# ScalarE's order inside a graph-attention step: the scalings of one chunk ahead of the exponentials of the next, and outputs one slot later

## The chip, the core and the metric

The kernel runs on one NeuronCore of one Trainium2 chip. The metric is the time on the device of one execution, in microseconds (us). A NeuronCore has five engines, each with its own queue that it works through in order: TensorE (PE: matrix products; PEld is the loading of its stationary operand), VectorE (DVE), ScalarE (ACT), GpSimd (POOL) and SyncE (SP). They meet only at semaphores. An engine whose next instruction waits holds up everything behind it in its own queue, and nothing else directly.

## The reference, cut to what matters

The input is `x`, 8 graphs of 2048 nodes with 128 features each, and one adjacency matrix of 2048 x 2048 with about 16 neighbours in a row. Four layers follow each other. Layers 0 and 1 are transformer layers whose attention is masked by the adjacency. Layers 2 and 3 are graph-attention (GAT) layers, and the change is in these:

```python
h = x @ W
s_i = h @ a_src
s_j = h @ a_dst
e = s_i[:, :, None] + s_j[:, None, :]
e = jnp.where(e >= 0, e, NEG_SLOPE * e)
e = jnp.where(adj[None, :, :] == 0, -jnp.inf, e)
att = jax.nn.softmax(e, axis=-1)
out = jnp.einsum('bij,bjd->bid', att, h)
y = out + x
mu = jnp.mean(y, axis=-1, keepdims=True)
var = jnp.mean((y - mu) ** 2, axis=-1, keepdims=True)
return ln_gamma * (y - mu) * jax.lax.rsqrt(var + LN_EPS) + ln_beta
```

For each node: a leaky-ReLU score for every neighbour, a softmax over the neighbours, the weighted sum of their rows `h`, the residual, and a layer norm.

## The kernel before, in words

**Lists and tables.** The adjacency is turned once into lists of neighbours. Nodes are sorted by their number of neighbours and cut into 16 tiles of 128 nodes (one a partition); tile t has `CAPS[t]` places for neighbours, from 30 down to 11, 277 in all. Each layer has a table in DRAM with one row a node: for a GAT layer the 8 graphs' `h` (8 x 128 values) and 8 scores `s_j`, 4128 bytes. One gather (line 296, an indirect DMA that POOL issues) brings one neighbour of each of 128 nodes into a buffer, so a GAT layer makes 277 gathers.

**Chunks.** A tile's neighbours are cut into chunks of 3 or 4 (`ns`; one chunk has 2), 75 chunks a GAT layer. A chunk's gathers fill one of `KVB = 6` buffers and are issued `AHEAD = 3` chunks early. The generator `gat_chunk` works off one chunk in five stages, divided by `yield`:

1. PE makes the scores `e` in one of three banks of PSUM (tag `m`): lines 654, 658, 662, the last of which reads the gathered `s_j` and so waits for the chunk's DMAs. ACT then makes two small exponentials of them, `wa` (line 667) and `wb` (line 668).
2. DVE takes the larger of the two as the weights, twice: line 670 into PSUM (`pair`) for itself and line 675 into SBUF (`ws`) for ACT.
3. The rows are scaled by their weights: DVE does 6 of the 8 graphs in one instruction (line 681), ACT the other two (`SCALED = 2`), in 2 x ns small instructions (line 686).
4. DVE folds the chunk's neighbours in half by one addition (line 690).
5. PE adds what is left into the tile's sums `acc`, with matmuls against the identity (line 696, four of 512 columns).

**Tails.** When a tile's last chunk is added, `sums` makes the softmax denominators, and `tail` starts a generator that passes some slots, divides on DVE (`outputs`, line 565, which reads `acc` and writes `o`), and starts two `gat_tail`s, one for each half of the graphs, the second three slots after the first. A `gat_tail` advances one `yield` a slot: PE makes the residual sum `y` (lines 706, 710, 714); `normed` takes ACT squares (line 404), a power on POOL (line 409, the reciprocal root), and, two slots after the squares, four ACT products (line 413). In layer 2 four PE transposes follow (line 305), one slot later an ACT copy (line 723), and one slot later `project`: PE makes the rows of the next table from the copy (lines 444, 450, 454, 459), and one slot later ACT copies them out (lines 464 to 466); when both halves are done, POOL scatters the rows into layer 3's table (`put_rows`, line 417). In layer 3 DVE applies the last gain and offset instead (lines 731, 732), and POOL scatters the result to the output (line 734).

**The order.** No scheduler moves anything: the kernel is recorded under a manual schedule, so each engine's queue holds its instructions in the order in which this Python code makes them. The loop in `layer` runs one iteration a chunk, i. For a GAT layer an iteration fetches chunk i+3, runs stage 1 of chunk i+1, stage 3 of chunk i-1, a slot, stage 2 of chunk i, a slot, stages 4 and 5 of chunk i-2, and a slot. `slot()` advances every tail by one step. So the order of an engine's queue in one iteration is: on PE, scores (i+1), tail steps of two slots, sums (i-2), tail steps of the third slot; on ACT, exponentials (i+1), scalings (i-1), tail steps of all three slots; on DVE, line 681 (i-1), lines 670 and 675 (i), line 690 (i-2), with `outputs` after that in the third slot; on POOL, the gathers (i+3), then the powers and scatters of the tails.

Of the kernel before, what the change touches and what calls it, by code (L numbers as in the profile page):

```python
# [51 lines left out]
def pieces(t, n):  # L52

    res, k = [], 0
    for m in split(CAPS[t] if t > 0 else BASE, n):
        res.append((k, m, False))
        k += m
    if t == 0:
        res.insert(1, (BASE, FOLD, True))
    return res  # L60
# [3 lines left out]
def sparse_path(ctx: ExitStack, tc: tile.TileContext, ins: dict, out: bass.AP, flag: bass.AP):  # L64
# [19 lines left out]
    def misc():  # L84
        return pm.tile([P, 512], F32, tag="m", name="m")
# [289 lines left out]
    def folded_sums(w, box):  # L375

        columns = w.shape[-1]
        ps = misc()[:, :columns]
        for i in range(FOLD):
            nc.tensor.matmul(ps, merge, w[:, i, :], start=i == 0, stop=i == FOLD - 1)  # L380
        box["folded"] = small.tile([P, columns], F32, tag="folded", name="folded", bufs=1)
        nc.scalar.copy(box["folded"], ps)
# [261 lines left out]
    def gat_chunk(l, c):  # L644
        box, t, k, ns = c["box"], c["t"], c["k"], c["ns"]
        if k == 0:
            box["acc"] = pacc.tile([P, NB // 4, 512], F32, tag="acc", name="acc")
            at, n = (0 if t % 2 == 0 else 512 - NB * CAPS[t]), CAPS[t]
            box["w"] = pair[:, at : at + NB * n].rearrange("p (s b) -> p s b", b=NB)
        acc, w = box["acc"], box["w"]  # L650
        hs = c["buf"]
        e = misc()[:, : ns * NB].rearrange("p (s b) -> p s b", b=NB)
        at = first[t] + k
        nc.tensor.matmul(
            e, ident_bf, lmask_bf[:, at : at + ns, None].to_broadcast([P, ns, NB]),
            start=True, stop=False,
        )
        nc.tensor.matmul(
            e, spread if c["folded"] else ident, s_own[:, t, None, :].to_broadcast([P, ns, NB]),
            start=False, stop=False,  # L660
        )
        nc.tensor.matmul(e, ident, hs[:, :, NB * D :], start=False, stop=True)  # L662

        wc = w[:, k : k + ns, :]
        wa = small.tile([P, 4, NB], F32, tag="wa", name="wa", bufs=3)
        wb = small.tile([P, 4, NB], F32, tag="wb", name="wb", bufs=3)
        nc.scalar.activation(wa[:, :ns, :], e, AF.Exp)  # L667
        nc.scalar.activation(wb[:, :ns, :], e, AF.Exp, scale=SLOPE)  # L668
        yield
        nc.vector.tensor_max(wc, wa[:, :ns, :], wb[:, :ns, :])  # L670
        if c["folded"]:
            box["wf"] = small.tile([P, FOLD, NB], F32, tag="wf", name="wf", bufs=1)
            nc.vector.tensor_max(box["wf"], wa[:, :ns, :], wb[:, :ns, :])
        ws = small.tile([P, 4, SCALED], F32, tag="ws", name="ws", bufs=3)
        nc.vector.tensor_max(
            ws[:, :ns, :], wa[:, :ns, NB - SCALED :], wb[:, :ns, NB - SCALED :]
        )
        yield
        hv = hs[:, :, : NB * D].rearrange("p s (b c) -> p s b c", b=NB)
        nv = NB - SCALED  # L680
        nc.vector.tensor_mul(  # L681
            hv[:, :, :nv, :], hv[:, :, :nv, :], wc[:, :, :nv, None].to_broadcast([P, ns, nv, D])
        )
        for i in range(ns):
            for b in range(nv, NB):
                nc.scalar.mul(hv[:, i, b, :], hv[:, i, b, :], ws[:, i, b - nv : b - nv + 1])  # L686
        yield
        left = -(-ns // 2)
        if ns > 1:
            nc.vector.tensor_add(hv[:, : ns - left], hv[:, : ns - left], hv[:, left:ns])  # L690
        yield
        if c["folded"]:
            folded_sums(box["wf"], box)
        for i in range(left):
            for j in range(NB // 4):
                nc.tensor.matmul(  # L696
                    acc[:, j, :], merge if c["folded"] else ident, hv[:, i, 4 * j : 4 * j + 4, :],
                    start=k + i == 0, stop=c["last"] and i == left - 1,
                )
        yield  # L700
# [230 lines left out]
    def advance(group):  # L931
        for g in list(group):
            if next(g, 0) == 0:
                group.remove(g)

    def slot():
        advance(threads)
        advance(tails)
# [5 lines left out]

    def tail(l, t, box):
        def rest():
            for _ in range(2 if l < 2 else 3):
                yield
            outputs(l, t, box)
            part = attention_tail if l < 2 else gat_tail  # L950
            tails.append(part(l, t, box, 0))
            tails.append(later(3, lambda: part(l, t, box, 4)))
            yield

        tails.append(rest())

    def later(n, make):
        for _ in range(n):
            yield
        yield from make()  # L960

    def layer(l):
        boxes = [{} for _ in range(NT)]
        att = l < 2
        per = 2 if att else 4
        chunks = []
        for t in range(NT):
            for k, ns, folded in pieces(t, per):
                chunks.append(dict(t=t, k=k, ns=ns, folded=folded, box=boxes[t], last=False))
            chunks[-1]["last"] = True  # L970
        n = len(chunks)

        def fetch(c):
            if c >= n:
                return
            c = chunks[c]
            c["buf"] = buffer()[:, : c["ns"] * width(l)].rearrange("p (s c) -> p s c", s=c["ns"])
            for i in range(c["ns"]):
                gather(l, first[c["t"]] + c["k"] + i, c["buf"][:, i])

        def state(t):
            if t < NT:
                if l == 0:
                    threads.append(fetch_state(t, boxes[t]))
                else:
                    boxes[t].update(x=load_state(t), ready=True)

        for box in boxes:
            box["state"] = state

        def begin(t):
            if att:
                threads.append(attention_begin(l, t, boxes[t]))

        if l == 0:
            threads.append(find_lists(0))
            state(0)
            drain()
        for i in range(AHEAD):
            fetch(i)  # L1000
        if l > 0:
            state(0)
        drain()
        begin(0)
        drain()
        if l == 0:
            threads.append(find_lists(1))
        run = [(attention_chunk if att else gat_chunk)(l, c) for c in chunks]

        def go(i, times=1):  # L1010

            if 0 <= i < n:
                for _ in range(times):
                    next(run[i], None)

        def is_last(i):
            return 0 <= i < n and chunks[i]["last"]

        def end(i):
            t = chunks[i]["t"]  # L1020
            tail(l, t, chunks[i]["box"])

        if not att:
            go(0)
        for i in range(n + 2):
            fetch(i + AHEAD)
            if i < n and chunks[i]["k"] == 0:
                t = chunks[i]["t"]
                if l == 0 and t + 2 < NT:
                    threads.append(find_lists(t + 2))  # L1030
                if t == 0:
                    state(1)
                    threads.append(later(12, lambda: state(2) or iter(())))
                while att and "asked" not in chunks[i]["box"]:
                    advance(threads)
            if i + 2 < n and chunks[i + 2]["k"] == 0:
                begin(chunks[i + 2]["t"])
            if att:

                go(i - 2)  # L1040
                if is_last(i - 2):
                    end(i - 2)
                go(i)
                slot()
                go(i)
                slot()
                if is_last(i - 1):
                    sums(l, chunks[i - 1]["t"], chunks[i - 1]["box"])
                go(i - 1, 2)
                slot()  # L1050
            else:


                go(i + 1)
                if is_last(i - 1):
                    sums(l, chunks[i - 1]["t"], chunks[i - 1]["box"])
                go(i - 1)
                slot()
                go(i)
                slot()  # L1060
                go(i - 2, 2)
                if is_last(i - 2):
                    end(i - 2)
                slot()
        if l == 3:
            verdict()
        drain()
# [530 lines left out]
```

## Time and profile before

| what | us |
|---|---|
| four runs | 3474.96, 3484.71, 3486.73, 3487.9; median 3485.72 |
| the profiled execution, its own time | 3481.77 |
| its span on the core (first to last instruction) | 3480.0 |
| busy in the span: DVE / PE / POOL / ACT | 3032.7 / 2827.8 / 2113.1 / 1450.3 |
| layer 2, first line 670 to last line 690 | 2343.0 to 2869.9 |
| layer 3, the same | 2921.0 to 3443.0 |

The first row is what a change is measured against; the profile is of one further execution. Layers 0 and 1 take the time before 2340 us, and the change does not touch them. Between the two GAT layers and after the second lie some 50 and 37 us in which the last tails run out and the next table is written.

In the lists of waits, "A <- B: t, n, m" says that instructions of line A stood idle t us in all before they started, n times, m us at most, and that B was the last thing they waited for; "issue" is idle time that ended with no event the profile shows. A timeline row gives the start, the duration, engine, line, operation, tiles and shapes, a count if several are merged, and in brackets the idle time before it. The figures of windows are busy times of each engine in a stretch; PEclk is the share of full TensorE clock that was granted.

### The profile page before, as it was taken

What the parts mean: (1) busy time and instruction counts of PE and PEld (TensorE: products, weight loads), DVE (VectorE), ACT (ScalarE), POOL (GpSimd) and SP (SyncE); (2) the same over time, 40 slices, a digit from 0 to 9 for tenths busy, and PEclk for the clock granted to TensorE, in tenths of its full rate; (3) what the DMA queues carried; (4) which work ended last, traced back from release to release, by engine and by line L of the source; (5) the groups of instructions that cost most, each with busy time, mean ns of one, the idle gap of its engine ahead of it and who ended that gap; (6) DMA issues with size and microseconds to landing.
All of it is one profiled execution on the core that took longest, in us unless ns stands there. A gap on an engine that the chain in (4) does not pass through costs nothing. (4 is left out here: it accounts for less than half of the span.)

```text
span 3480.0 us, 36421 instructions
## 1 busy us (share of the span) xinstructions
PE 2827.8 (81%) x11364; PEld 1676.2 (48%) x11364; DVE 3032.7 (87%) x2545; ACT 1450.3 (42%) x5142; POOL 2113.1 (61%) x1441
## 2 busy tenths in 40 slices
PE   5657888889899966888888999967898896877786
PEld 4423454455555542445555555653555554444443
DVE  8789999999999929999999999928777773988886
ACT  5712333344444430223333434444555553444454
POOL 0054666666666433655677766528877755888874
PEclk9879999999999989989999999988999997889888
DMA  8486788888787557777887887728998865888883
GB/s 338 181 304 247 276 298 302 322 289 306 296 318 292 195 198 269 275 300 280 302 313 293 303 304 291 258 96 282 318 311 307 321 215 203 293 305 291 293 274 123
DMA packets 195892, 955.38 MB, mean 275 GB/s; under 512 B 33778, under 2 KB 35572, under 8 KB 124080
## 3 DMA queue, kind: packets, MB, share of 16 engines
q0 software_dynamic: 172352, 859.22, 68.6%
q1 hardware_dynamic: 18434, 75.51, 5.7%
q10 hardware_dynamic: 4904, 18.24, 1.4%
q8 instruction: 93, 1.52, 0.2%
q14 instruction: 109, 0.89, 0.1%
HBM read 934.86 MB, written 85.07 MB: 293 GB/s over the span
## 5 line engine op out<-in xcount | busy, mean ns | idle before, releaser
L296 POOL DMA_INDIRECT kv<-table,lists x1108 | 1612.9, 1456 | 549.0 <-issue 228.2
L546 PE MATMUL acc<-kv,ident 128*128 128x512 f32 x2200 | 1105.9, 633 | 260.7 <-DVE kv L536 260.2
L546 PEld LDWEIGHTS acc<-kv,ident 128*128 128x128 f32 x2200 | 411.9, 201 | 699.1 <-issue 365.8
L522 DVE TENSOR_TENSOR kv<-kv,q 128x2048 f32<-128x2048 f32 (+1 forms) x282 | 629.3, 2231 | 71.4 <-DMA kv<-table,lists 64.0
L525 DVE TENSOR_REDUCE sc<-kv 128x128 f32<-128x2048 f32 (+1 forms) x284 | 634.1, 2233 | 9.4
L409 POOL TENSOR_TENSOR rs<-ss,half 128x4 f32<-128x4 f32 x192 | 321.4, 1674 | 516.9 <-ACT n L404 510.4
L536 DVE TENSOR_TENSOR kv<-kv,w 128x2048 f32<-128x2048 f32 (+1 forms) x284 | 631.4, 2223 | 0.0
L696 PE MATMUL acc<-kv,ident 128*128 128x512 f32 x1184 | 601.9, 656 | 14.3 <-DVE kv L690 13.5
L404 ACT ACTIVATE n<-m,eps 128x128 f32<-128x128 f32 x768 | 271.5, 369 | 479.4 <-PE m L628 219.0
L681 DVE TENSOR_TENSOR kv<-kv,pair 128x3072 f32<-128x3072 f32 (+1 forms) x150 | 465.2, 3101 | 0.0
L531 ACT ACTIVATE w<-sc,lmask 128x64 f32<-128x64 f32 x554 | 164.4, 348 | 528.9 <-DVE sc L525 412.3
L690 DVE TENSOR_TENSOR kv<-kv 128x2048 f32<-128x2048 f32 (+1 forms) x150 | 296.6, 1978 | 84.0 <-ACT kv L686 62.9
L696 PEld LDWEIGHTS acc<-kv,ident 128*128 128x128 f32 x1184 | 238.9, 213 | 268.4 <-issue 227.3
L686 ACT ACTIVATE kv<-kv,ws 128x128 f32<-128x128 f32 x1108 | 339.0, 397 | 0.1
L413 ACT ACTIVATE n<-m,rs 128x128 f32<-128x128 f32 x768 | 218.3, 368 | 101.7 <-POOL rs L409 101.1
L667 ACT ACTIVATE wa<-m 128x32 f32<-128x32 f32 (+1 forms) x150 | 29.4, 196 | 485.0 <-PE m L662 424.9
L662 PE MATMUL m<-kv,ident 128*128 128x32 f32 (+1 forms) x300 | 62.2, 290 | 169.1 <-DMA kv<-table,lists 158.6
L404 ACT ACTIVATION_READ_ACCUMULATOR n<-m,eps 128x1 f32 x768 | 159.4, 208 | 0.0
L670 DVE TENSOR_TENSOR pair<-wa,wb 128x32 f32<-128x32 f32 (+1 forms) x150 | 29.8, 199 | 145.8 <-ACT wb L668 118.2
L628 PE MATMUL m<-w_L_w,hT 128*128 128x128 f32 x1024 | 156.3, 275 | 0.0
L417 POOL DMA_INDIRECT table<-rows,perm x48 | 78.0, 1625 | 111.6 <-ACT rows L441 51.1
L305 PE MATMUL m<-ident,n 128*128 128x128 f32 x640 | 108.7, 288 | 32.6 <-ACT n L413 30.2
(217 smaller groups left out, 3531.2 us busy)
## 6 DMA issues: line engine op xcount, KB each, us to landing
kept<-xT SPq DMA_DIRECT2D x48, 512.0 KB
xT<-kept SPq DMA_DIRECT2D x48, 512.0 KB
kv<-table,lists POOLq DMA_INDIRECT x1108
kv<-in_adj_dram SPq DMA_DIRECT2D x16, 1024.0 KB
table<-kv ACTq DMA_DIRECT2D x16, 1024.0 KB
kv<-in_x_nodes_dram SPq DMA_DIRECT2D x16, 512.0 KB
found<-cand POOLq DMA_DIRECT2D x16, 64.0 KB
table<-rows,perm POOLq DMA_INDIRECT x48
```

Source lines behind the costliest of these rows:

```text
L296: nc.gpsimd.indirect_dma_start(out=dst, out_offset=None, in_=tables[l][:, :], in_offset=bass.IndirectOffsetOnAxis(ap=lists[:, at : at + 1] ...
L404: nc.scalar.activation(dst[:, i, :], z[:, i, :], AF.Square, bias=eps, scale=D**-0.5, accum_out=ss[:, i : i + 1],)
L409: nc.gpsimd.tensor_tensor(rs, ss, half, op=ALU.pow)
L413: nc.scalar.mul(dst[:, i, :], z[:, i, :], rs[:, i : i + 1])
L522: nc.vector.tensor_mul(kk, kk, q[:, None].to_broadcast([P, ns, NB, D]))
L525: nc.vector.tensor_reduce(sc[:, :ns].rearrange("p s (b h) -> p (s b) h", h=NH), kk.rearrange("p s b (h j) -> p (s b) h j", h=NH), axis=AX. ...
L536: nc.vector.tensor_mul(vv, vv, w[:, k : k + ns, :].rearrange("p s (b h) -> p (s b) h", h=NH)[:, :, None, :] .to_broadcast([P, ns * NB, HD, ...
L546: nc.tensor.matmul(acc[:, j, :], merge if c["folded"] else ident, kv[:, i, 4 * j : 4 * j + 4, D:], start=k + i == 0, stop=c["last"] and i ...
L681: nc.vector.tensor_mul(hv[:, :, :nv, :], hv[:, :, :nv, :], wc[:, :, :nv, None].to_broadcast([P, ns, nv, D]))
L686: nc.scalar.mul(hv[:, i, b, :], hv[:, i, b, :], ws[:, i, b - nv : b - nv + 1])
L690: nc.vector.tensor_add(hv[:, : ns - left], hv[:, : ns - left], hv[:, left:ns])
L696: nc.tensor.matmul(acc[:, j, :], merge if c["folded"] else ident, hv[:, i, 4 * j : 4 * j + 4, :], start=k + i == 0, stop=c["last"] and i = ...
```

## The change

Two edits in what a GAT step does, and the calls that follow from them.

```diff
         nc.tensor.matmul(e, ident, hs[:, :, NB * D :], start=False, stop=True)
+        yield
 
         wc = w[:, k : k + ns, :]
...
-            for _ in range(2 if l < 2 else 3):
+            for _ in range(2 if l < 2 else 4):
                 yield
             outputs(l, t, box)
...
         if not att:
-            go(0)
+            go(0, 2)
...
                 go(i - 1)
+                go(i + 1)
                 slot()
                 go(i)
                 slot()
```

Stage 1 is cut in two: the scores on PE, and the exponentials on ACT. An iteration now runs the scores of chunk i+1, stage 3 of chunk i-1, the exponentials of chunk i+1, and then its slots. ACT's queue so has the scalings (line 686) ahead of the exponentials (lines 667, 668); PE's, DVE's and POOL's stages keep their places. And a GAT tile's `outputs` waits for four slots instead of three. It started in the third slot of an iteration; now it starts in the first slot of the next one. Every step of a GAT tail follows it by one slot. No instruction is added or removed, and no operand changes. Lines behind 663 get a number higher by one.

## The prediction

> **What bounds the kernel now.** The change touches only layers 2 and 3, so I read the profile by stage: first the windows of the two layers, then who waits for whom in each, then the timeline of one iteration. Windows (columns: busy us and count of PE, PEld, DVE, ACT, POOL; clock; DMA share; GB/s):
>
> ```profile
> 2343.00:2870.00 527.00, 455.27 (x1877) 268.46 (x1878) 420.41 (x381) 281.83 (x1150) 388.06 (x310) 0.93 0.84 293
> 2921.00:3443.00 522.00, 411.49 (x1277) 216.16 (x1277) 456.85 (x438) 253.40 (x1051) 413.49 (x325) 0.88 0.83 281
> ```
>
> No engine is full in either layer, so the waits decide. Waits of layer 2, first PE's, then DVE's, then ACT's longest (three lists of the same window):
>
> ```profile
> PE m L662 <- DMA kv<-table,lists: 34.7, 16, 6.7
> PE m L305 <- ACT n L413: 29.1, 23, 2.0
> ...
> PE m L305 <- ACT kv L686: 1.9, 3, 1.0
> ```
> ```profile
> DVE kv L690 <- ACT kv L686: 33.3, 19, 2.1
> DVE o L565 <- PE acc L696: 26.8, 12, 5.9
> DVE kv L690 <- issue: 9.8, 7, 2.1
> ```
> ```profile
> ACT wa L667 <- PE m L662: 196.4, 61, 7.7
> ```
>
> PE's busy 455 plus 35 for gathers plus 31 for ACT (29.1 + 1.9) is 521 of 527 us: **layer 2 is paced by PE**. 26 of the 35 us fall before 2430 us, while the first gathers fill up. DVE's idle 106 us are slack behind PE. In layer 3 it is POOL: busy 413, and its gathers have a further gap between them:
>
> ```profile
> POOL kv L296 <- issue: 57.3, 190, 1.7
> POOL rs L409 <- ACT n L404: 14.0, 6, 4.8
> ```
>
> The 57.3 us are 190 gaps of 0.3 us; the other gathers have the same gap under other names (some 30 us more). With the waits on ACT that is over 510 of 522 us. PE waits 91.3 us for gathers there: they come as fast as POOL issues them.
>
> One iteration of layer 2, from the timeline:
>
> ```profile
> 2617.60 0.18 PE L654 MATMUL m<-lmask_bf,ident_bf 128*128 128x32 bf16 x1
> ...
> 2618.28 0.20 ACT L667 ACTIVATE wa<-m 128x32 f32<-128x32 f32 x1 [2.46 <-PE m L662]
> 2618.29 1.05 PE L450 MATMUL m<-w_L_h,xT 128*128 128x128 f32 x8
> 2618.37 0.19 ACT L668 ACTIVATE wb<-m 128x32 f32<-128x32 f32 x1
> 2618.45 1.85 ACT L686 ACTIVATE kv<-kv,ws 128x128 f32<-128x128 f32 x6
> ...
> 2619.21 1.03 PE L459 MATMUL m<-w_L_h,xT 128*128 128x2 f32 x8
> ...
> 2620.20 1.12 ACT L413 ACTIVATE n<-m,rs 128x128 f32<-128x128 f32 x4
> ...
> 2621.38 1.11 PE L305 MATMUL m<-ident,n 128*128 128x128 f32 x4 [1.13 <-ACT n L413]
> ```
>
> Read it as a loop: PE makes scores; ACT, which had stood 2.46 us for them, runs its exponentials, then 1.85 us of scalings (2.44 for chunks of four), then the tail's products L413; PE waits for these with the transposes L305, and the sums L696 stand behind L305. The scalings were ready to run during the 2.46 us.
>
> **The change, part by part.** Sums are against the profiled execution's own 3481.8 us; the median of the runs shown is 3.9 us above.
>
> *1. L305's wait, layer 2: -31 us.* L413 loses 1.85 to 2.44 us of scalings ahead of it, and by the slot's shift L305 now stands behind L696 (eight passes, 3.44 us where the clock is full). Either alone covers a wait of 2.0 us at most. That the scalings fit in front: step by step in the trace, L667's idle time is longer than the block of L686 behind it in 62 of layer 2's 73 steps and in 47 of layer 3's; where it is not, the exponentials come up to 2.4 us later. Nobody is waiting for them there: L670 reads them an iteration later. The weights `ws` that L686 needs are always done, by 6.5 us at least before the present start of the exponentials.
>
> *2. A new wait, layer 2: +22 us.* The slot's shift also moves the copy L723 from the third slot (before the next scores) to the first (behind the next exponentials), and `project` reads that copy on PE right after the scores. From the rows: L654 starts at 0, exponentials at 0.68, ACT's next instruction at 0.85, the copy takes 0.60 and ends at 1.45; L450 starts 0.69 now and would start at about 1.5. That is 0.8 us for each of 28 halves in the window. Behind the waiting L450 stand L459, the sums L696 and the next scores; POOL's gathers wait for the buffers that L696 frees. Bounds: 0 if ACT runs far ahead, and 1.2 us a half (34 us) if `project`'s PSUM bank, which is that of the scores, holds back L444 too. I take 0.8, since each of its parts is a row.
>
> *3. DVE's waits: -3 us.* L690's waits (43 us) and L565's (27 us) go: L686 is done before the exponential that L670 waits for, and `outputs` stands 3.3 us (one L681) later. Both are hidden behind PE, whose L696 waits only 3.1 us for L690. What can come off is those 3 us; the bound is the 70 us in which DVE would be late if PE weren't.
>
> *4. TensorE's clock, layer 2: 0, between -10 and +10.* Three neighbouring windows round the L305 wait shown above:
>
> ```profile
> 2617.70:2621.10 3.40, 2.55 (x24) 2.42 (x22) 2.19 (x4) 2.82 (x12) 2.60 (x4) 1.00 0.91 317
> 2621.10:2624.50 3.40, 3.12 (x7) 1.92 (x8) 3.40 (x2) 1.41 (x5) 1.32 (x1) 0.51 0.96 342
> 2624.50:2627.90 3.40, 3.40 (x16) 1.88 (x15) 0.40 (x2) 0.38 (x3) 1.60 (x2) 0.99 0.84 284
> ```
>
> The clock halves for 3.4 us round a wait of 1.13 us, which costs up to 1.7 us. The old waits are longer (1.27 us each), the new ones more (28 for 23) and amid small matmuls; six windows either way are the 10 us. The Trainium skill (TensorE: Matmul & The Clock Gate, "What's actually happening") has the clock fall after an idle window of about 3.4 us; by it neither the old nor the new waits would touch the clock, and this term would be 0 without bounds. The row shows a halving with PE busy 2.55 of the 3.4 us before, so the bounds stay.
>
> *5. POOL and the buffers: -5 us.* In layer 2 POOL waits 23.4 us for L696 to free buffers; L696 comes ahead of L305 in two iterations a tile, but behind the new wait in two. The scatter L417 goes behind four gathers, and its wait of 7.4 us for ACT goes. Half of these 7.4 us, and 1 us of the rest: -5, between 0 and -15.
>
> *6. Layer 3: -4 us.* There is no L723 and no L305, so part 2 has no counterpart. POOL's gathers keep their number and length. What can go are its waits for ACT, 14.0 for L404 and 2.8 for L667: squares move a slot later but lose the scalings ahead of them. A quarter of 17; bounds -15, and +6 if the later slot makes the powers later. L731 and L732 move behind L681, 3.3 us later; their scatter L734 stands at least 5.0 us behind them in the layer now, so it is covered.
>
> *7. The ends: +1 us.* One slot more of the last tile but one runs after each loop. The `y` matmuls, one slot later, find `o` done: its new end is that of the present next L681, before or at their present start in every tile of layer 2's loop.
>
> Sum: -31 + 22 - 3 + 0 - 5 - 4 + 1 = -20. Parts 1 and 5 partly count the same time (a PE that is earlier frees buffers earlier anyway), so I take **-16**: 3466 on the profiled execution's terms, and 3468 against the runs, whose median is a little above it.
>
> **Rivals.**
>
> *A, larger gain:* DVE's and ACT's waits were what kept gathers late, so most of the 43 us of L690 goes too. For: the layer's DMA share is only 0.84. Against: L696 waits 3.1 us for L690. 3482 - 45 = 3437.
>
> *B, nothing:* L450's wait takes L305's place in full. This decides from 31 / 28 = 1.1 us a half, against my 0.8; with layer 3 at 0, 3482 to 3485. For it: the PSUM bank.
>
> *C, slower:* the copy comes later than I have it, because ACT is still in the scalings when the scores are done: those are now in front of the exponentials and the copy. If it costs 2 us a half, layer 2 gets 56 - 31 = 25 us longer, and with the clock's 10 some 35: 3517. It decides from 1.1 us a half too, and B ends where C begins. For: the full tail iterations, where ACT has squares and copies in the third slot. Against: 62 of 73 steps with room.
>
> *D, the change doesn't do what it says:* the built program's order shows L686 ahead of L667 and L305 behind L696, so I give it none.
>
> **How the numbers follow.** Forecast 0.48, A 0.13, B 0.25, C 0.14. The forecast's own spread is 3452 to 3478 by the bounds of parts 2, 4 and 5. About 0.3%, 10.5 us, is what a measurement of this kernel can tell from no change: faster is under 3475, slower over 3496. Faster: 0.40 of the forecast, A, and nothing else, 0.53. Same: the rest of the forecast, most of B, 0.31. Slower: C and 0.02 of B, 0.16. The range 3436 to 3496 takes in the forecast, A and B, and leaves C out.
>
> **What would show it.** L305's wait gone; L450 <- ACT L723 new, about 0.8 us x 28 in layer 2; L690 <- L686 and L565 <- L696 gone; L670 <- L668 not grown; layer 2 some 12 us shorter, layer 3 about the same. I am wrong if PE's waits in layer 2 sum to what they did, if the clock of layer 2 (0.93) moves by more than 0.02, or if layer 3 moves by more than 15 us.

## The result, and the profile after

The changed kernel takes 3487.82 us in the median (3479.45 to 3503.68, 41 runs), the kernel before 3485.52 (3472.18 to 3497.91, 67 runs): a ratio of 1.0008, 95% interval 1.0002 to 1.0014. The change moves nothing that matters. The profiled execution after took 3482.28 us, with a span of 3480.5.

Layer 2, from the first line 671 to the last line 691, went from 526.8 to 520.8 us; layer 3 from 522.0 to 522.5. Layer 2 began 4.3 us later though nothing ahead of it was changed (it began between 2340.0 and 2347.5 us in every kernel below but e20). With 1.4 us more between the two layers, this takes up the 6 us by which layer 2 is shorter. Each kernel has one profiled execution, and layer 3 took 522.5 to 533.7 us in four kernels whose layer 3 is the same (after, e21, e24 and e26). So single layers are read below to some 10 us, and kernels by their ratios. The windows of layers 2 and 3 after (columns as before):

```profile
2347.00:2868.00 521.00, 453.94 (x1857) 266.77 (x1856) 417.06 (x381) 287.48 (x1149) 397.35 (x311) 0.93 0.85 295
2921.00:3443.00 522.00, 403.14 (x1275) 214.47 (x1275) 450.23 (x435) 253.22 (x1047) 417.77 (x325) 0.89 0.83 281
```

PE is busy 454 us where it was busy 455, at the same clock of 0.93: nothing was won there. What PE waited for in layer 2:

```profile
PE m L662 <- DMA kv<-table,lists: 44.8, 26, 6.2
PE m L450 <- ACT xT L724: 6.1, 10, 0.6
PE m L444 <- ACT wb L669: 5.1, 9, 1.0
PE m L662 <- issue: 4.1, 3, 2.9
...
PE m L305 <- ACT n L413: 1.2, 1, 1.2
```

The wait of the transposes is gone, 31.0 to 1.2. In its place stand `project`'s waits, 15.6 us with the smallest rows (for the copy at L450; at L444 for a bank that the exponentials free, which are later now), and a longer wait for gathers, 48.9 us with the row marked "issue" where it was 36.4. Idle on PE in all: 71.7 before, 66.9 after. That is an exchange, not a gain.

The part of the gathers' wait in which the layer starts up is the same, 25.8 us before (up to 2430 us) and 25.5 after (up to 2434). The rest grew from 10.6 to 23.4. The same two rows behind the start-up, before and then after:

```profile
PE m L662 <- DMA kv<-table,lists: 8.9, 7, 2.0
PE m L662 <- issue: 1.7, 3, 1.2
```
```profile
PE m L662 <- DMA kv<-table,lists: 19.3, 17, 2.2
PE m L662 <- issue: 4.1, 3, 2.9
```

Issuing the gathers also kept GpSimd busy 19 us longer, for the same number of them (groups of layer 2, before and after; behind the count stand busy us and mean ns):

```profile
L296 POOL DMA_INDIRECT kv<-table,lists x269 | 329.5, 1225 | 105.3 <-issue 55.0 <-PE acc L696 23.4 <-PE m L658 9.1
L296 POOL DMA_INDIRECT kv<-table,lists x270 | 348.4, 1290 | 102.0 <-issue 60.2 <-PE acc L697 27.1 <-ACT wb L669 2.7
```

### The profile page after: what moved, and what is told of

The parts are those of the page before. It is cut to its first block, busy times and chain, and to the rows that moved or that the text cites. A ratio compares the mean times of both kernels' runs of the same rounds, so it can differ in the third digit from the quotient of the medians.

```text
span 3480.5 us, 36448 instructions
## 1 busy us (share of the span) xinstructions
PE 2817.8 (81%) x11364; PEld 1672.5 (48%) x11364; DVE 3023.9 (87%) x2545; ACT 1456.9 (42%) x5142; POOL 2134.5 (61%) x1441
## 5 line engine op out<-in xcount | busy, mean ns | idle before, releaser
L296 POOL DMA_INDIRECT kv<-table,lists x1108 | 1638.8, 1479 | 541.2 <-issue 237.9
L691 DVE TENSOR_TENSOR kv<-kv 128x2048 f32<-128x2048 f32 (+1 forms) x150 | 296.0, 1973 | 1.3 <-ACT kv L687 1.3
L671 DVE TENSOR_TENSOR pair<-wa,wb 128x32 f32<-128x32 f32 (+1 forms) x150 | 29.8, 199 | 249.9 <-ACT wb L669 155.6
L668 ACT ACTIVATE wa<-m 128x32 f32<-128x32 f32 (+1 forms) x150 | 29.4, 196 | 350.9 <-PE m L662 314.8
L662 PEld LDWEIGHTS m<-kv,ident 128*128 128x128 f32 x300 | 49.5, 208 | 204.1 <-issue 168.3
L628 PEld LDWEIGHTS m<-w_L_w,hT 128*128 128x128 f32 x1024 | 135.0, 192 | 0.0
```

The lines of the kernel that those rows point to most:

```text
L296: nc.gpsimd.indirect_dma_start(out=dst, out_offset=None, in_=tables[l][:, :], in_offset=bass.IndirectOffsetOnAxis(ap=lists[:, at : at + 1] ...
L628: nc.tensor.matmul(y[:, j, :], hT[:, f, j, :], wt["2"][:, f, :], start=False, stop=f == 1, skip_group_check=True,)
```

## The experiments

Three theories stood first. **T1**: GpSimd's queue of gathers paces both layers, so nothing on PE matters. **T2**: TensorE paces layer 2, and `project`'s new wait took the place of the transposes'. **T3**: the two edits cancel, and each alone does much. Later ones are **P** (the copy's wait is what the slot's shift costs) against **O** (the earlier half of the tail, outputs to powers, is), **G** (GpSimd's gathers hold the changed kernel back, in a second form because late sums reach their queue through the buffers), and **K** (the cost is TensorE's clock) against **W** (the waits themselves).

All runs in one table. Each ratio is to runs of the kernel before that were taken with it (medians 3483 to 3488), so rows are compared by their ratios; e4, e5 and e23 rest on two runs each. The last four columns are us of layer 2 in the profiled execution: its length, PE's busy and idle time, which add up to it, and the time at half clock in the stretches that begin in it. One more such stretch, begun before the layer, covers its first 15 to 19 us in each run, 35 in e3.

| kernel | us (median) | ratio to before, 95% | layer 2 | PE busy | idle | half |
|---|---|---|---|---|---|---|
| before | 3485.5 | 1 | 526.8 | 455.2 | 71.7 | 51 |
| after | 3487.8 | 1.0002 to 1.0014 | 520.8 | 453.9 | 66.9 | 55 |
| e1 order only | 3458.5 | 0.9896 to 0.9928 | 498.6 | 442.4 | 56.1 | 38 |
| e2 slot only | 3601.1 | 1.0304 to 1.0332 | 644.6 | 530.1 | 114.5 | 229 |
| e3 half the sums | 3449.3 | one run | 499.2 | 374.1 | 125.1 | 137 |
| e4 before, fewer gathers | 3409.1 | 0.9748 to 0.9794 | 504.3 | 447.9 | 56.4 | 38 |
| e5 after, fewer gathers | 3369.4 | 0.9662 to 0.9701 | 470.2 | 433.9 | 36.3 | 17 |
| e10 after, copy first | 3477.2 | 0.9975 to 0.9996 | 511.9 | 451.0 | 60.9 | 61 |
| e11 late half shifted | 3471.2 | 0.9954 to 0.9986 | 513.1 | 449.5 | 63.6 | 48 |
| e26 early half shifted | 3489.8 | 1.0003 to 1.0027 | 520.8 | 448.3 | 72.4 | 61 |
| e24 after, copy unread | 3474.4 | 0.9962 to 0.9986 | 510.3 | 444.7 | 65.6 | 51 |
| e28 slot only, copy unread | 3482.2 | 0.9979 to 1.0008 | 515.4 | 451.3 | 64.1 | 61 |
| e20 slot only, filled | 3560.4 | 1.0190 to 1.0229 | 561.3 | 504.0 | 57.3 | 31 |
| e23 slot only, half filled | 3557.4 | 1.0178 to 1.0230 | 584.4 | 506.0 | 78.4 | 106 |
| e21 after, filled | 3483.8 | 0.9979 to 0.9999 | 516.9 | 457.6 | 59.3 | 38 |
| e22 before, filled | 3493.4 | 1.0003 to 1.0026 | 530.1 | 473.6 | 56.5 | 34 |
| e16 after, rows reversed | 3482.2 | 0.9982 to 1.0018 | 515.4 | 452.5 | 62.9 | 55 |
| e17 order, rows reversed | 3459.5 | 0.9935 to 0.9972 | 500.5 | 439.2 | 61.3 | 31 |
| e18 before, rows reversed | 3483.6 | 0.9992 to 1.0018 | 527.5 | 457.7 | 69.8 | 58 |
| e19 e10, rows reversed | 3477.6 | 0.9973 to 1.0001 | 507.7 | 446.6 | 61.1 | 51 |

Layer 3 lay between 522 and 534 us in all of them but e4 and e5, with no order among the edits: the kernel before with only layer 2 edited (e22) had 529.

### One edit at a time, and each engine's load

e1 keeps the `yield` and the calls `go(0, 2)` and `go(i + 1)`, and undoes the slot; e2 is the reverse.

```diff
-            for _ in range(2 if l < 2 else 4):
+            for _ in range(2 if l < 2 else 3):
```

> The scalings go ahead of the exponentials, outputs stay in the third slot. Theory T1 (POOL's queue of gathers paces both GAT layers, so time saved on ScalarE and TensorE is slack): within 0.1% of before, layer 2 within 6 us of 527. Theory T2 (TensorE paces layer 2, and in the full change the wait of project for the copy took the place of the transposes' wait): here the copy stays in the third slot, so there is no such wait, the transposes' wait of 31 us shrinks to under 5, and the time falls by 15 to 30 us. Theory T3 (the two edits cancel): this one is faster by 10 us or more.

> Outputs one slot later, the order on ScalarE as before. The copy now stands behind the scalings: by the rows of before, project on TensorE waits 2.9 us a half, 81 us in layer 2. T1: some of that hides behind the gathers, layer 2 grows by 0 to 40 us. T2: layer 2 grows by 81 - 31 = 50 us. T3: the time grows by 10 us or more, as much as the order alone gains.

e3 and e4 lighten one engine of the kernel before:

```diff
-        for i in range(left):
+        for i in range(1):
...
-                    start=k + i == 0, stop=c["last"] and i == left - 1,
+                    start=k + i == 0, stop=c["last"],
```

> Before, with only the first of a chunk's two row sums added by TensorE (line 696), so half of its summing matmuls in the GAT layers is left out: TensorE loses 130 us in each of layers 2 and 3. T1: layer 2 loses under 25 us and layer 3 under 10, since the gathers go on as they were. T2: layer 2 loses 50 us or more.

```diff
-            for i in range(c["ns"]):
+            for i in range(c["ns"] - (l > 1 and c["ns"] == 4)):
```

> Before, with the fourth gather of each chunk of four left out in the GAT layers (53 of 277 a layer; the chunk is worked off with what lies in the buffer). T1: POOL loses 53 x 1.55 = 82 us a layer, and both layers get shorter by 40 us or more, until TensorE (486 us with its waits in layer 2) or VectorE (457 us busy in layer 3) takes over. T2: layer 2 loses under 15 us, layer 3 40 us or more.

**T3 holds, and strongly.** Against the kernel before, the order alone is 31 us faster, the slot alone 112 us slower, and together they make nothing. PE's waits in layer 2 with the order alone, and with the slot alone:

```profile
PE m L662 <- DMA kv<-table,lists: 39.8, 20, 5.6
PE m L305 <- ACT n L413: 14.5, 11, 3.0
```
```profile
PE m L450 <- ACT xT L723: 66.2, 27, 3.0
PE m L662 <- DMA kv<-table,lists: 37.8, 17, 6.3
```

And PE's wait for gathers in e3, where PE has less to do:

```profile
PE m L662 <- DMA kv<-table,lists: 83.0, 40, 5.9
```

The order alone already takes half of the transposes' wait away (31 to 14.5; T2 had expected under 5). The slot alone puts 66 us of `project`'s wait in, since ACT there has the exponentials *and* the scalings ahead of the copy. Layer 3 is a matter of gathers (e4: 471 us; e3: 525), as I had it. So T1 is right there. Layer 2 answers to both (499 in e3, 504 in e4): it has two bounds close to each other, and T1 and T2 have half of it each.

### The same lightening after the change

> The changed kernel, and in both GAT layers the fourth gather of chunks of four is left out (the rows of an older chunk stand in its place); the pair of the same edit on the kernel before, which took 3409 us with 504 us in layer 2 and 471 in layer 3. Theory P: with gathers out of the way layer 2 is paced by TensorE alone, whose waits for ScalarE are 15 us in place of 31, so layer 2 takes 485 to 495 and the kernel 3390 to 3400. Theory G (GpSimd's gathers hold the changed kernel back, since they are late and longer): layer 2 falls by more than 35 us, under 486, and the kernel under 3390. Theory O: layer 2 504 or more, 3409 or more. Layer 3 471 by all.

The edit is that of e4. It took 3369 us, with layer 2 in 470.2: only G, in its first form, allowed that much. With a fourth of the long chunks' gathers left out, the change is worth 34 us in layer 2 (504.3 to 470.2) and 31 in the kernel by the two ratios (0.9771 and 0.9681; 40 by the medians). PE's waits, first of e4, then of e5:

```profile
PE m L305 <- ACT n L413: 29.3, 27, 1.7
PE acc L696 <- DVE kv L690: 19.5, 15, 2.7
PE m L662 <- DMA kv<-table,lists: 7.7, 2, 4.9
```
```profile
PE m L662 <- DMA kv<-table,lists: 10.7, 7, 5.0
PE m L450 <- ACT xT L724: 8.7, 14, 0.6
PE acc L697 <- DVE kv L691: 7.7, 6, 2.1
PE m L444 <- ACT wb L669: 5.6, 13, 1.0
```

Parts 1 and 3 of the prediction, the waits of L305 and of DVE, come off here. In the changed kernel with all its gathers, PE spends a part of what it wins waiting for them. The gathers alone don't force that: the order alone has all of them too, in a layer of 499 us, with 40 us of waiting for them.

### Do late sums hold up the gathers?

After the change GpSimd waits 27.1 us in layer 2 for the sums to free a buffer. A chunk's rows behind the half are free earlier, once DVE's addition has read them; so e16 (after), e17 (order only), e18 (before) and e19 (e10) issue a chunk's gathers last row first:

```diff
-            for i in range(c["ns"]):
+            for i in range(c["ns"]) if l < 2 else reversed(range(c["ns"])):
```

> The changed kernel, and in the GAT layers the gathers of a chunk are issued last row first. The rows behind the half are free when DVE's addition L691 has read them, so a chunk's first gathers no longer wait for the sums L697 on TensorE, and two or one gathers lie between a late sum and GpSimd's queue. Nothing else moves. Theory G (GpSimd's queue, gathers and powers, paces the changed kernel's layer 2, and the late sums reach it through the buffers): the waits of L296 for L697, 27 us in layer 2, fall under 10 us, layer 2 falls from 521 to 495 to 505, and the kernel takes 3452 to 3470. Theory P (TensorE's own queue paces it, with project's waits for the copy in it): the gathers come earlier but layer 2 stays at 515 or more, the kernel at 3478 to 3490.

> The kernel before, with the gathers of a chunk issued last row first in the GAT layers; all else as it was. The pair of the same edit on the changed kernel. In layer 2 L296 waits 23 us for L696 here too. Theory G with TensorE beside it as the second bound (half of the sums left out gave 499 us, a fourth of the gathers left out 504): layer 2 falls from 527 to no less than 504, since TensorE's waits of 31 us for the products stay: 505 to 518, the kernel 3463 to 3475. If GpSimd's queue alone paced it: 495 to 503, below 3462. If TensorE alone: 520 or more, 3478 or more.

> The order alone (scalings ahead of the exponentials, outputs in the third slot as before the change), with the gathers of a chunk issued last row first. There L296 waits only 5 us for L697, and GpSimd is busy 399 of layer 2's 499 us with some 95 us of gaps between its instructions. Theory G: nothing is left to win in layer 2, 493 to 500 us, and the kernel takes 3450 to 3460, so that with the rows reversed it and the changed kernel come within 10 us of each other. Theory P: it stays 20 us or more ahead of the changed kernel with the same edit.

> The changed kernel with the copy L724 ahead of the exponentials and the gathers of a chunk issued last row first. Theory G: as for the changed kernel with the rows reversed, 495 to 505 us in layer 2 and 3452 to 3470, within 5 us of it, since the copy's wait costs only by way of the buffers. Theory P: 10 us or more under it, since the copy's wait costs on TensorE itself.

**G's second form falls.** GpSimd's waits in layer 2, after and in e16:

```profile
POOL kv L296 <- PE acc L697: 27.1, 34, 3.5
POOL rs L409 <- ACT n L404: 10.4, 2, 5.6
```
```profile
POOL rs L409 <- ACT n L404: 11.9, 2, 7.1
POOL kv L296 <- PE m L658: 9.8, 8, 3.4
POOL kv L296 <- PE acc L697: 4.0, 5, 2.7
```

The wait for the sums went as expected, 27.1 to 4.0, and none of the four kernels became clearly faster than its pair (e16 has 1.0000 for 1.0008, with intervals that overlap; e17 is 0.4% slower than e1 by the ratios). PE's wait for gathers did fall in e16, from 48.9 to 39.8 us, and rose in e17, from 40.1 to 48.6. So neither this wait nor GpSimd's sets the time by itself.

### Which part of the slot's shift costs: the copy, or the earlier half of the tail?

e10 exchanges only two things on ACT: the first slot, with the copy, comes ahead of the exponentials.

```diff
                 go(i - 1)
-                go(i + 1)
                 slot()
+                go(i + 1)
                 go(i)
```

> The changed kernel with one exchange on ScalarE: an iteration's first slot, which holds the copy L724, comes ahead of the exponentials L668 and L669 and no longer behind them. No other engine's order moves. Theory P (project's wait for the late copy takes back what the order of the scalings gave): L450's and L444's waits, 11 us in layer 2 of the changed kernel, fall under 3 us, layer 2 falls from 521 to some 500 us, which is the length that the order alone gave, and the kernel takes 3455 to 3466. Theory O (the rest of the slot's shift costs it: outputs, squares, powers and scatters a slot later): layer 2 stays within 5 us of 521 and the kernel at 3478 to 3490.

The wait for the copy did not go in e10, it moved: L444 needs a bank that the copy frees, and stands 9.3 us for it.

```profile
PE m L444 <- ACT xT L724: 9.3, 12, 2.9
```

e11 is the order alone with one `yield` more ahead of `transpose4`, e26 the changed kernel with one `yield` fewer between squares and products in layer 2; together they halve the shift.

> The order alone (outputs in the third slot as before the change), and one slot more ahead of the transposes L305: outputs, squares, powers and products stay where they were before the change, while transposes, copy and project stand where the changed kernel has them. Theory P: L450 waits for the copy again, some 10 us or more in layer 2, layer 2 goes from 499 back to 515 to 521, and the kernel takes 3475 to 3488. Theory O: the early half of the tail keeps the gain, 3455 to 3465, layer 2 at some 500.

> The changed kernel with one slot fewer between the squares and the products in layer 2: outputs, y, squares and powers stand a slot later, as in the changed kernel, while products, transposes, copy and project stand where the order alone has them. On ScalarE this differs from the order alone in one exchange (copy ahead of squares), on TensorE in the place of y. Theory P: layer 2 495 to 503, 3455 to 3465, the waits for the transposes back at some 15 us. Theory O: 510 to 521, 3470 to 3488. The run with only the later half shifted gave 513, so by a plain sum of halves 507.

e24 takes the copy's wait away at its source, and e28 does the same to the slot alone:

```diff
-            nc.scalar.copy(xT[:, i : i + 4, :], pt)
+            nc.scalar.copy(work.tile([P, 4, P], F32, tag="nT", name="turned"), pt)
```

> The changed kernel, whose copy L724 goes to a tile that nobody reads; project reads the state as it was loaded, so layer 3's table is not the reference's. All instructions and their order stay; only project's wait for the copy goes. Theory P (that wait, with the clock behind it, is what the shift takes back): layer 2 falls from 521 to 495 to 507, L450's waits under 1 us, the kernel at 3455 to 3470. Theory O (the earlier half of the tail takes it back): L450's waits go too, but layer 2 stays at 511 or more, the kernel at 3473 to 3488.

> The slot's shift alone, with the copy L723 going to a tile that nobody reads, as above. Theory K (wait and clock are the whole cost of the slot's shift): the waits of 66 us and the 25 stretches at half clock at L450 go, and since L305's wait of 29 us is gone there too, layer 2 falls from 645 to 495 to 525, at or under the 527 of the kernel before. Rival (the shift costs elsewhere as well, by ScalarE's order or the sums): 535 to 600.

PE's waits in e28, then in e24, then in e26:

```profile
PE m L662 <- DMA kv<-table,lists: 37.7, 19, 5.9
PE m L454 <- ACT turned L723: 17.2, 13, 1.7
```
```profile
PE m L662 <- DMA kv<-table,lists: 55.6, 30, 5.6
PE m L444 <- ACT wb L669: 6.9, 10, 2.5
```
```profile
PE m L662 <- DMA kv<-table,lists: 33.9, 17, 6.7
PE m L305 <- ACT n L413: 32.9, 14, 5.4
```

For the slot alone the copy's wait, with the clock behind it, is the whole cost: without it layer 2 takes 515 us in place of 645, and the kernel is level with the one before. In the changed kernel it is a part only. Without it (e24) the kernel gains 0.34% by the two ratios, some 12 us, of the 0.96% or 33 us that lie between after and the order alone; e10 gains 8 us. In e24 the gathers' wait rises to 55.6, so PE again waits for gathers with part of what it won. Both halves of the shift cost: the late half alone (e11) takes back some 20 us of the 33, the early half alone (e26) all of it, by another wait (the transposes wait 32.9 us for the products, which here have a slot less between them and the squares). So neither P nor O alone is right, and the halves don't add.

### Is it the wait, or TensorE's clock behind it?

The slot alone lost 118 us in layer 2 with 66 us of new wait. A half of its tail in the timeline of PE:

```profile
2789.79 0.38 PE L444 MATMUL m<-parts_h,ones_bf 128*128 128x512 bf16 x1 [0.37 <-ACT wb L668]
2792.59 1.95 PE L450 MATMUL m<-w_L_h,xT 128*128 128x128 f32 x8 [2.42 <-ACT xT L723]
...
2796.11 5.40 PE L696 MATMUL acc<-kv,ident 128*128 128x512 f32 x8
```
```profile
2789.30:2792.70 3.40, 0.61 (x4) 0.14 (x4) 2.98 (x4) 3.24 (x13) 2.98 (x3) 1.00 0.67 188
2792.70:2796.10 3.40, 3.40 (x17) 3.34 (x18) 3.40 (x2) 1.46 (x5) 2.79 (x3) 0.51 0.63 168
```

The clock (the third figure from the end of a window's row) falls from 1.00 to 0.51 at the end of a wait of 2.42 us. Behind it `project`'s eight passes take 1.95 us where the prediction's timeline showed 1.05, and the sums 5.40 where they take 3.4 at full clock. Filling such a wait with matmuls leaves what is waited for as late as it was, but keeps PE busy. e20, e23 and e21 issue `project`'s first matmul 12, 6 and 4 times:

```diff
-            nc.tensor.matmul(
-                pp, ones_bf, w["bias"][:, None, :D].to_broadcast([P, 4, D]),
...
+            for _ in range(12):
+                nc.tensor.matmul(
+                    pp, ones_bf, w["bias"][:, None, :D].to_broadcast([P, 4, D]),
...
```

> The slot's shift alone (which took 3601 us, 645 in layer 2), and project's first matmul L444 is issued 12 times in place of once (each starts the sum anew, so the result is the same). Project's wait for the copy, 1.6 to 3.0 us in each of 27 halves, is filled with some 2.3 us of matmuls; nothing is waited for less. Theory K (the clock: in layer 2 it stood at half for 229 us, 25 of 31 such stretches beginning at this wait): the waits L450 <- ACT L723 shrink from 66 to under 20 us, stretches at half clock fall under 12, L696's eight passes go back from 5.7 to 3.4 us, layer 2 falls to 545 to 575 and the kernel to 3500 to 3530, with 60 us more work on TensorE. Theory W (the waits themselves cost, by what stands behind them): layer 2 stays within 15 us of 645, the kernel at 3590 to 3615.

> As the last, with L444 issued 6 times: some 1.1 us of matmuls in a wait of 1.6 to 3.0 us, so that 0.5 to 1.9 us of waiting stay. Theory K: between the two; the halves whose wait stays above about 1 us still halve the clock, 8 to 20 such stretches, the kernel 3530 to 3580. Theory W: 3590 to 3615.

> The changed kernel with L444 issued 4 times in place of once: some 0.64 us of matmuls in front of project's wait for the copy, 0.46 to 0.64 us in half of the halves. Theory K: the four or five stretches at half clock that begin at L444 or L450 go, 4 x 3.4 to 7 us x 0.5 = 7 to 14 us less TensorE time, against up to 10 us of filling where there was no wait; layer 2 505 to 520, the kernel 3468 to 3485. Theory W: layer 2 521 to 535, 3483 to 3500.

e22 puts five such matmuls into the transposes' bank, ahead of L305, in the kernel before:

```diff
         pt = misc()
+        for _ in range(fill):
+            nc.tensor.matmul(
+                pt.rearrange("p (b c) -> p b c", c=D), ones_bf,
+                W[3]["bias"][:, None, :D].to_broadcast([P, 4, D]),
+                start=True, stop=True, skip_group_check=True,
+            )
```

> The kernel before, with five matmuls of 512 columns in layer 2 into the bank that the four transposes L305 are about to overwrite: 1.1 us of filling in L305's waits for the products (0.45 to 2.0 us in 27 of 28 halves). What is waited for stays as late as it was. Theory K: 10 of layer 2's 13 stretches at half clock begin at this wait and go, some 40 us x 0.5 = 20 us less TensorE time, less some 6 us of filling beyond the wait: layer 2 507 to 520, the kernel 3460 to 3475, so a good part of what the order alone gains comes from the clock. Theory W: layer 2 525 to 540, 3480 to 3495.

The same place in e20 (line numbers one higher), and its layer 2:

```profile
2773.96 2.75 PE L445 MATMUL m<-parts_h,ones_bf 128*128 128x512 bf16 x12 [0.37 <-ACT wa L668]
2776.77 1.16 PE L451 MATMUL m<-w_L_h,xT 128*128 128x128 f32 x8
...
2778.69 3.68 PE L697 MATMUL acc<-kv,ident 128*128 128x512 f32 x8
```
```profile
2374.00:2936.00 562.00, 504.54 (x2157) 287.75 (x2156) 421.14 (x381) 286.48 (x1149) 386.48 (x310) 0.96 0.82 273
```

**K holds for the slot alone.** With more work on PE, layer 2 is 83 us shorter (644.6 to 561.3), the time at half clock falls from 229 to 31 us, and PE is busy *less*, 504 us for 530. Filled by half, it lies between (584.4). The kernel missed its expected time, 3560 for 3500 to 3530, since layer 2 began 34 us later than in e2: `project` with its 12 matmuls also runs in the tails of layer 1, which write layer 2's table, a thing that the expectation had left out. In the changed kernel (e21) the clock's part is small: half clock 55 to 38 us, layer 2 521 to 517, the kernel 0.2% faster than after by the two ratios. e22, with 530 us and 3493, lies in W's ranges, but its edit missed: the bank that its matmuls need is often the one that the products themselves free (19.4 us of the wait stand ahead of the filling), so it added some 30 us of work for 17 us less at half clock, and does not decide between K and W for the kernel before.

## Why the prediction was wrong

The forecast of 3468 was wrong; rival B, nothing, came true, though not by the mechanism that I gave it.

- *Part 1* (L305's wait, -31): right in size, -29.8. But half of it, and a gain of 31 us in the kernel, belongs to the order alone; the slot's shift removed only the other 13 us.
- *Part 2* (`project`'s wait, +22): the wait came, and smaller, 15.6 us. So B's condition, 1.1 us a half, was not met: L450's and L444's waits together were 0.56 us a half.
- **The step that failed** is the sum itself: it takes what PE no longer waits at L305 off the time one for one, and has no term for the wait for gathers, which it so put at nothing without a reason. That wait went from 36.4 to 48.9 us. Idle on PE in layer 2: transposes -29.8, sums -3.9, `project` +15.6, gathers +12.5, which makes -5.6 against -4.8 measured. Without the gathers' +12.5 the layer would by this sum have come out some 18 us shorter, near the forecast. The reading "26 of the 35 us while the first gathers fill up" was right, and these 26 us stayed; what grew is the rest, 10.6 to 23.4, and it is as large in three other kernels that keep the whole shift (25.6 in e10, 25.3 in e21, 30.1 in e24). "Paced by PE" was only half of it: with half of PE's sums left out, the wait for gathers grows to 87 us and the layer takes 499 (e3); with fewer gathers the change does gain 34 us in the layer (e4, e5). But that this wait is what takes the gain back is not shown: with the rows reversed the changed kernel has 39.8 us of it and is no faster than before (e16), and the order alone has 48.6 and keeps most of its gain (e17). The prediction's own sign of failure, that PE's waits sum to what they did, did appear: 71.7 and 66.9 us, closer than layers can be told apart.
- *Part 3* (DVE, -3) and *part 5* (GpSimd and buffers, -5): L690's wait went, as expected, and L565's more than halved (26.8 to 11.9); PE's wait for L690 fell by 3.1, and rival A's further 45 us did not come. DVE's wait for the exponentials (`L670 <- L668`), which was not to grow, grew from 77.4 to 105.3 us. The issue of a gather, for which no part had a term in layer 2, became longer (1225 to 1290 ns in the mean). L296's wait for the sums rose instead of falling, 23.4 to 27.1, and in e16, almost without it, the kernel was not clearly faster.
- *Part 4* (clock, 0 between -10 and +10): right for the sum (0.93 and 0.93), by compensation. Ten of 13 stretches at half clock began at L305's wait before; after, seven of 11 begin at the gathers' wait and four at `project`. The bounds were needed: with the order alone the clock is worth some 7 us of layer 2 (half of 51 less 38), with the slot alone half of 229 less 51, 89 us. The Trainium skill (TensorE: Matmul & The Clock Gate, "HAM oscillation — how this bites in real kernels") asks for no idle gaps over about 3.4 us; no wait at `project` in e2 is longer than 3.0, and 21 of its 31 stretches at half clock begin at the wait for the copy there. The measurement decides: shorter waits do it.
- *Part 6* (layer 3, -4) and *7* (+1): +0.5 in the layer and +1.7 at the ends, within their spread.
- *Rival C* was right about its mechanism: behind the scalings, the copy costs 2.45 us a half (66.2 / 27), and the clock falls behind it. It is what the slot does without the new order. The two edits of the change are not independent: the order is what makes the slot bearable, and the slot is what spoils the order.

What stays open: of the 33 us between the changed kernel and the order alone, some 12 go with the copy's wait (e24), clock included. In the two profiles layer 2 differs by 22 us: PE is idle 10.8 us longer, and busy 11.5 us longer with the same matmuls. The clock (55 us at half for 38) makes some 9 of these 11.5. In the idle time `project`'s 15.6 us and 8.8 us more for gathers stand against 13.3 us less at the transposes. The late gathers go with GpSimd's wait for the sums in the changed kernel (48.9 to 39.8 us in e16), and yet e16 gains next to nothing; taking the copy's wait away makes them later still (e24, 56.1). Why the rest is lost when outputs, squares and powers stand a slot later was not found.

The version to keep is the order alone: 3458.5 us, 0.9912 of before (0.9896 to 0.9928), and the rows reversed (e17) add nothing to it.

## What to carry to other kernels

Measure a change of two edits edit by edit before believing that it does nothing: here a gain of 31 us was hidden under a cost. When the busiest engine's waits are counted as gains, ask what it will wait for next, and by how much; split such a wait into its start-up and the rest, since here 26 us stayed and the rest more than doubled. And price a wait on TensorE by its length and by what the clock does behind it.

## What the runs showed of the hardware

TensorE's clock fell to half at waits for the copy of 1.8 to 3.0 us in e2 (21 of 31 falls) and at waits of L305 of 1.1 to 2.0 us in the kernel before (10 of 13), amid steady work, and at times stayed there for more than one step of 3.41 us (e2: 229 us in 31 stretches, 7.4 each). In layer 2 of the 20 kernels in the table all 247 falls followed a step of 3.41 us in which the trace has PE busy for less than 87%, in e2 half of them some 31% or less; no step that was busier was followed by a fall, while some of 42 to 75% were not followed by one either. In e2 66 us of wait cost 129 us of layer 2 by e28, in which 17 us of another wait took their place, and matmuls of no use put into the wait brought 83 of them back.

In layer 2 a gather's issue on GpSimd took 1.0 us, but some took up to 3.1. Every issue above 1.15 us (46 of 268 before, 55 after) ended 0.86 to 0.94 us after the end of one of DVE's additions (L690, in the changed kernel L691). In all they took 60 us more than 1.0 us each before, and 78 after.
